# A second attention's threshold, search, product and loop order, rewritten

## The chip, the cores and the metric

The kernel runs on one core of one Trainium2 chip. The metric is device time in microseconds (us) of one execution, given as the median of several. All times, durations and waits below come from those runs or from one profiled execution of the kernel before.

The core has five engines that run beside each other, each through its own list of instructions in order: PE (TensorE, matrix products; its weight loads are listed apart as PEld), DVE (VectorE), ACT (ScalarE), POOL (GpSimd) and SP (SyncE, which here issues the transfers). [...] An instruction waits on semaphores for the results that it reads and for the space that it writes.

## What is computed

A graph of 1250 nodes with 512 features goes through a first graph layer, a first attention with experts, a second graph layer and a second attention. Only the second attention is changed. Its reference, cut to what matters:

```python
qkv = x @ qkv_w.T + qkv_b            # x: one sequence of 1250 rows, with positions added
q, k, v = jnp.split(qkv, [c, 2 * c], axis=-1)
q, k, v = (_split_heads(t, h) for t in (q, k, v))          # 8 heads of 64
logits = jnp.einsum('bmd,bpd->bmp', qd * scale, kd)
_, idx = lax.top_k(logits, TOPK)                           # TOPK = 16
k_sel, v_sel = gather(k, idx), gather(v, idx)
attn = jax.nn.softmax(jnp.einsum('bmd,bmkd->bmk', q * scale, k_sel), axis=-1)
out = jnp.einsum('bmk,bmkd->bmd', attn, v_sel)
...
return out @ wo_w.T + wo_b                                 # added to x
```

Each row of each head takes its sixteen largest of 1250 scores, and a softmax over those sixteen alone weighs the values.

## The kernel before

The first 1110 us of the execution hold the first three layers and the projections of the second attention. The change leaves them as they are. The second attention is a loop of 40 steps (`steps`): ten row tiles `i` of 125 rows, and for each four pairs `j` of heads. Within a step the two heads of the pair are a_ = 0 and a_ = 1. The order of the work is written out by hand, under `manual_schedule`: each engine runs its instructions in the order in which the loop's body calls the helpers. Three steps are in work at once: step n is scored and searched, step n-1 is weighted and transposed, step n-2 multiplies its values.

One head of one step goes this way:
- `scores1` (L1595): TensorE writes scores of 125 rows by 1250 columns into a PSUM tile S of three banks, in three pieces (512, 512 and 226 columns), two products each. There is one such tile for each a_, so the next step's scores can be written only when both readings by ScalarE (below) are through.
- `largest1` (L1602): VectorE searches S with fourteen MAX8 instructions, each over every fourteenth column (89 or 90), and keeps eight values of each: 112 candidates.
- `first1` (L1611, L1612): a MAX8 over the candidates gives the eight largest (`top[:, 0:8]`); `nm` is the negative of the largest.
- `weights1` (L1630): ScalarE writes e = exp(S - largest).
- `second1` (L1620 to L1624): the eight largest are replaced among the candidates, a second MAX8 gives ranks nine to sixteen, and `gap` and `below` make the threshold: the negative of the sixteenth score, raised by a margin of 2^-22 times the larger magnitude among ranks one and eight. `gap` and `below` each read two columns of SBUF.
- `select1` (L1637, L1640): ScalarE takes the sign of S + below (1 for the sixteen, -1 for the others; the sums of the signs are collected for a test at the end), and GpSimd multiplies e by it in place, all 1250 columns in one instruction.
- `turn1` and `keep1` (L1650, L1657): TensorE transposes the twenty 125x125 blocks of the two heads in five groups of four (group 2 holds two blocks of each head), and ScalarE copies each group out with a Relu, which sets the unwanted, now negative weights to zero.
- `values1`, `outputs1` (L1706, L1716): TensorE multiplies the transposed weights by the values, and ScalarE copies the result out.

Once in a row tile come other small works, spread over its four steps by c = n % 4: the sum of the sixteen exponentials and its inverse (`sums1` to `sums_keep1`, with `sums_over1` on VectorE, L1673 and L1674, and `sums_turn1` on TensorE, L1687), the scaling of the outputs (`scale1`, L1694, on GpSimd), the split of the next tile's queries into halves (`halves1`: ScalarE L1580, GpSimd L1581, two transfers on SP), and in each step a quarter of the output projection (`project1`, L1724, on TensorE), which `finish1` (L1732) adds to X on VectorE; a finished tile is sent out by a transfer on SP. Transposes, outputs, the projection and the sums' transposes share two PSUM banks (`ps_to1`), taken in turn.

In a step of before TensorE runs: value products of n-2 (first 0 to 8, in 32 recorded products), transposes 0 of n-1, the last value products, two score pieces of head 1, transposes 1, the last score piece of head 1, transposes 2, the projection, the first score piece of head 0 of n+1, transposes 3, its other two pieces, transposes 4. ScalarE runs: sign of head 1 (n-1), keep 0, outputs, exp of head 0, keep 1, sign of head 0, keep 2, halves or the sums' exp, keep 3, exp of head 1, keep 4. VectorE runs: search, `first1`, `second1` of head 0, then search, `finish1`, `first1`, `second1` of head 1. GpSimd runs the two products and the works named above.

Of the kernel before, what the change touches and what calls it, by code (L numbers as in the profile page):

```python
# [9 lines left out]
F32 = mybir.dt.float32  # L10
# [6 lines left out]
ALU = mybir.AluOpType  # L17
# [555 lines left out]
def tile_usual(ctx: ExitStack, tc: tile.TileContext, a: dict, out: bass.AP):  # L573
# [970 lines left out]


    TINY = 2.0 ** -22
    SEARCHED = 14
    wo_pool, wo_p = pool("wo", 1)
    w_o = wo_p.tile([128, K, D], F32, name="w_o1")
    nc.sync.dma_start(w_o, a["wo"].rearrange("(k p) f -> p k f", p=128))  # L1550
# [2 lines left out]
    with (  # L1553
# [42 lines left out]
                                     start=(x == 0), stop=(x == 1))  # L1596


        def largest1(n, a_):
            largest[n, a_] = at1.tile([P, SEARCHED, 8], F32, tag=f"largest{a_}", name="largest")  # L1600
            for k in range(SEARCHED):
                nc.vector.max(out=largest[n, a_][:, k, :], in_=score[n, a_][:, k:N:SEARCHED])  # L1602

        def first1(n, a_):
            i, j = steps[n]
            h = 2 * j + a_
            if h == 0:
                bests[i] = at1.tile([P, H, TOPK], F32, name="best")
            top = bests[i][:, h, :]
            nm = maxima[n, a_] = at1.tile([P, 1], F32, tag=f"nm{a_}", name="nm1")  # L1610
            nc.vector.max(out=top[:, 0:8], in_=largest[n, a_].rearrange("p g e -> p (g e)"))  # L1611
            nc.vector.tensor_scalar(nm, top[:, 0:1], -1.0, None, op0=ALU.mult)  # L1612

        def second1(n, a_):
            i, j = steps[n]
            top = bests[i][:, 2 * j + a_, :]
            gap = at1.tile([P, 1], F32, tag=f"gap{a_}", name="gap")
            below = belows[n, a_] = at1.tile([P, 1], F32, tag=f"below{a_}", name="below")
            rest = at1.tile([P, SEARCHED * 8], F32, name="rest")
            nc.vector.match_replace(out=rest, in_to_replace=top[:, 0:8],  # L1620
                                    in_values=largest.pop((n, a_)).rearrange("p g e -> p (g e)"), imm_value=LOWEST)
            nc.vector.scalar_tensor_tensor(gap, top[:, 7:8], -1.0, top[:, 0:1], op0=ALU.mult, op1=ALU.max)  # L1622
            nc.vector.max(out=top[:, 8:16], in_=rest)
            nc.vector.scalar_tensor_tensor(below, gap, TINY, top[:, 15:16], op0=ALU.mult, op1=ALU.subtract)  # L1624

        def weights1(n, a_):
            if n > last:
# [5 lines left out]
        def select1(n, a_):  # L1633
            if not 0 <= n <= last:
                return
            sg = at1.tile([P, N], F16, tag=f"sg{a_}", name="sg", bufs=1)
            nc.scalar.activation(sg, score.pop((n, a_))[:, :N], AF.Sign, bias=belows.pop((n, a_)),  # L1637
                                 accum_out=signs[:, 2 * n + a_ : 2 * n + a_ + 1])
            e = es[n, a_]
            (nc.vector if 2 * n + a_ == 2 * last + 1 else nc.gpsimd).tensor_mul(e, e, sg)  # L1640

        def turn1(n, g):
            if not 0 <= n <= last:
                return
            if g == 0:
                pTs[n] = at1.tile([P, 2 * T, P], F32, name="pT1")
            turned[n, g] = ps_to1.tile([128, 512], F32, tag="to", name="ps_t1")
            g0, g1 = GROUPS[g]
            for b in range(g0, g1):
                nc.tensor.transpose(turned[n, g][:P, span(b - g0, b - g0 + 1)],  # L1650
                                    es[n, b // T][:, span(b % T, b % T + 1)], ident[:P, :P])
# [41 lines left out]
        def scale1(i):  # L1693
            nc.gpsimd.tensor_mul(oTs[i], oTs[i], sums.pop(i))  # L1694

        def values1(n, t0, t1):
            if not 0 <= n <= last:
                return
            i, j = steps[n]
            if t0 == 0:  # L1700
                outs[n] = ps_to1.tile([128, 512], F32, tag="to", name="O")
            pT = pTs[n]
            for t in range(t0, t1):
                for a_ in range(2):
                    h = 2 * j + a_
                    nc.tensor.matmul(outs[n][a_ * DH : (a_ + 1) * DH, :P],  # L1706
                                     V[:, t, h * DH : (h + 1) * DH], pT[:, a_ * T + t, :],
                                     start=(t == 0), stop=(t == T - 1))
# [54 lines left out]
        with tc.manual_schedule():  # L1763
            nc.sync.dma_start(w_v, a["qkv"][:, 2 * D :].rearrange("(k p) f -> p k f", p=128))
            nc.sync.dma_start(v_b, bass.AP(tensor=a["v_b"].tensor, offset=a["v_b"].offset, ap=[[0, P], [1, D]]))
            for a_ in range(2):
                halves1(0, a_)
            scores1(0, 0, 0, 2, 1)
            for n in range(len(steps)):


                i, c = n // K - 1, n % K
                if i >= 0 and c == 3:
                    scale1(i)
                select1(n - 1, 1)
                largest1(n, 0)
                values1(n - 2, 0, 5)
                first1(n, 0)
                if n == 1:
                    keep_late1()  # L1780
                second1(n, 0)
                values1(n - 2, 5, 8)
                turn1(n - 1, 0)
                keep1(n - 1, 0)
                values1(n - 2, 8, T)
                scores1(n, 1, 1)
                scores1(n, 1, 0)
                outputs1(n - 2)
                if i >= 0 and c == 1:
                    sums_over1(i)  # L1790
                weights1(n, 0)
                if i >= 0 and c == 2:
                    sums_turn1(i)
                    sums_keep1(i)
                turn1(n - 1, 1)
                scores1(n, 1, 2)
                if n < 2:
                    values_late1(T - 3 + 2 * n)
                keep1(n - 1, 1)
                turn1(n - 1, 2)  # L1800
                if i >= 0 and c == 0:
                    sums1(i)
                if i >= 1:
                    project1(i - 1, c)
                select1(n, 0)
                largest1(n, 1)
                keep1(n - 1, 2)
                finish1()
                if c < 2:
                    halves1(steps[n][0] + 1, c)  # L1810
                if i >= 0 and c == 1:
                    sums_wide1(i)
                scores1(n + 1, 0, 0)
                if i >= 0 and c == 0:
                    sums_exp1(i)
                if n == 1:
                    keep_late1()
                turn1(n - 1, 3)
                keep1(n - 1, 3)
                first1(n, 1)  # L1820
                if n == 0:
                    keep_late1()
                scores1(n + 1, 0, 2)
                scores1(n + 1, 0, 1)
                if n == 0:
                    values_late1(T - 2)
                weights1(n, 1)
                turn1(n - 1, 4)
                keep1(n - 1, 4)
                second1(n, 1)  # L1830

            n, i = len(steps), T - 1
            sums1(i)
            values1(n - 2, 0, 5)
            select1(n - 1, 1)
            turn1(n - 1, 0)
            values1(n - 2, 5, T)
            keep1(n - 1, 0)  # L1840
            outputs1(n - 2)
            sums_exp1(i)
            turn1(n - 1, 1)
            keep1(n - 1, 1)
            sums_over1(i)
            sums_wide1(i)
            y0 = ps_s1a.tile([P, 3 * 512], F32, name="S")
            y1 = ps_s1b.tile([P, 3 * 512], F32, name="S")
            project1(i - 1, 0, D, y0[:, :D])
            turn1(n - 1, 2)  # L1850
            keep1(n - 1, 2)
            finish1()
            sums_turn1(i)
            sums_keep1(i)
            turn1(n - 1, 3)
            keep1(n - 1, 3)
            R = sums.pop(i)
            oT = oTs[i]
            nc.vector.tensor_mul(oT[:, : K - 1, :], oT[:, : K - 1, :], R[:, : K - 1, :])

            def terms(*ks):
                for k in ks:
                    nc.tensor.matmul(y1[:, :D], oT[:, k, :], w_o[:, k, :], start=(k == 0), stop=(k == K - 1))

            terms(0)
            turn1(n - 1, 4)
            signs_over1()
            terms(1)
            keep1(n - 1, 4)
            values1(n - 1, 0, T)  # L1870
            terms(2)
            nc.vector.tensor_mul(oT[:, K - 1, :], outs.pop(n - 1)[:, :P], R[:, K - 1, :])
            terms(K - 1)
            projected.append((i, slice(0, D), y1[:, :D]))
            finish1()
# [62 lines left out]
```

## Time and profile before

| | |
|---|---|
| median of 3 runs | 1533.59 us (1533.37 to 1535.1) |
| the profiled execution: its own time | 1535.23 us |
| its span | 1533.3 us |
| mean granted TensorE clock | 0.987 |
| from 1110 to 1512 us (402 us): PE, PEld busy | 367.5, 296.6 us |
| the same stretch: DVE, ACT, POOL busy | 380.6, 334.5, 243.9 us |

In a row of groups the profile gives line, engine, operation, what is written from what, shape and count; then the busy time of the group (overlaps counted once) and the mean duration of one; then the engine's idle time just before it and what ended it. In a timeline a row gives the start, the length and the count of merged instructions. Instructions of one engine overlap a little in it: the next one may start before the last one's end. A row of stretches gives busy time and count for each engine in turn. The busy share is an average over instructions that may stand still while they count as busy, and the ends of matrix products are modelled.

### The profile page before, as it was taken

How to read it: one execution, taken by the hardware profiler on the slowest of the kernel's cores; microseconds unless marked ns; L12 is line 12 of the kernel's file. 1: busy time of each engine (PE TensorE's matmuls, PEld its weight loads, DVE VectorE, ACT ScalarE, POOL GpSimd, SP SyncE). 2: the span in 40 equal slices, each digit the busy share in tenths (PEclk: the TensorE clock that was granted, in tenths of full speed). 3: DMA queues.
4: the chain of work that ended last, by engine and by line, in shares of the span. 5: the costliest groups of instructions: out<-in, count | busy, mean ns of one | idle time of the engine just before them, and what ended most of it. 6: DMA issues, size and time to landing. Idle time of an engine off the chain costs nothing.

```text
span 1533.3 us, 22442 instructions
## 1 busy us (share of the span) xinstructions
PE 1429.5 (93%) x8127; PEld 938.3 (61%) x8127; DVE 913.7 (60%) x2772; ACT 708.0 (46%) x1351; POOL 350.2 (23%) x301
## 2 busy tenths in 40 slices
PE   5999999979999998999999999989888999999997
PEld 3666744457777775444444446654467777777775
DVE  8895567544444332412222434654599999999995
ACT  2333434455455552211000123431178888888884
POOL 0110000001111120000000122210046666666652
PEclk9999999989999999999999999999999999999999
DMA  4001000010101000210000100000200000000000
GB/s 138 29 1 55 1 0 1 4 48 15 42 16 48 21 24 14 60 54 28 28 28 28 50 7 28 1 28 0 75 15 14 15 22 22 22 22 22 22 8 23
DMA packets 42331, 41.19 MB, mean 27 GB/s; under 512 B 25738, under 2 KB 30084, under 8 KB 42211
## 3 DMA queue, kind: packets, MB, share of 16 engines
q1 hardware_dynamic: 42211, 39.66, 9.0%
q8 instruction: 66, 1.08, 0.3%
q14 instruction: 54, 0.44, 0.1%
HBM read 26.81 MB, written 2.56 MB: 19 GB/s over the span
## 4 chain that ended last, share of the span: by engine, by line
PE 59%; DVE 30%; ACT 8%; issue 2%; DMA 0%; POOL 0%; DVEq 0%; ACTq 0%; SPq 0%
PE ps_o L1334 9%; DVE largest L1602 9%; PE ps_mm L1326 7%; DVE gap L1622 5%; PE ps_mm L865 5%; PE ps_mm L800 5%; PE S L1034 4%; PE ps_mm L1462 4%; PE ps_o L870 4%; PE ps_t L1122 4%; PE O L1143 3%; PE bank L768 2%; PE O L1187 2%; DVE below L1624 2%; PE S L1157 1%
## 5 line engine op out<-in xcount | busy, mean ns | idle before, releaser
L1640 POOL TENSOR_TENSOR e<-e,sg 125x1250 f32<-125x1250 f32 x79 | 203.3, 2573 | 157.2 <-ACT sg L1637 105.6
L1602 DVE MAX8 largest<-S 125x8 f32<-125x89 f32 (+1 forms) x1120 | 183.3, 239 | 3.8 <-PE S L1595 3.8
L1336 DVE SCALAR_TENSOR_TENSOR X<-ps_o,gate,X 125x512 f32<-125x512 f32 x80 | 60.0, 750 | 177.0 <-PE ps_o L1334 177.0
L1595 PE MATMUL S<-K,stacks 128*125 128x512 f32 x480 | 135.7, 394 | 24.5 <-ACT sg L1637 19.0
L1650 PE MATMUL ps_t<-ident,e 125*125 125x125 f32 x800 | 136.3, 288 | 14.1 <-POOL e L1640 6.8
L1650 PEld LDWEIGHTS ps_t<-ident,e 125*125 125x125 f32 x800 | 111.9, 191 | 48.5 <-ACT pT L1657 14.5
L1334 PE MATMUL ps_o<-we,hid 128*125 128x512 f32 x320 | 141.2, 595 | 0.0
L1657 ACT ACTIVATE pT<-ps_t 125x500 f32<-125x500 f32 x200 | 117.0, 585 | 33.6 <-PE ps_t L1650 31.7
L1329 ACT ACTIVATE hid<-ps_mm,b 128x500 f32<-128x500 f32 (+1 forms) x40 | 24.6, 614 | 209.0 <-PE ps_mm L1326 209.0
L1326 PE MATMUL ps_mm<-yT,we 128*128 128x500 f32 (+1 forms) x320 | 115.8, 520 | 0.0
L1630 ACT ACTIVATE e<-S,nm 125x1250 f32<-125x1250 f32 x80 | 104.1, 1302 | 18.1 <-DVE nm L1612 17.9
L1637 ACT ACTIVATE sg<-S,below 125x1250 f16<-125x1250 f32 x80 | 104.4, 1305 | 16.4 <-DVE below L1624 12.9
L1706 PE MATMUL O<-pT,yT 125*64 125x125 f32 x1600 | 105.0, 276 | 0.2 <-ACT pT L1657 0.2
L1334 PEld LDWEIGHTS ps_o<-we,hid 128*125 128x125 f32 x320 | 59.0, 187 | 72.4 <-issue 69.6
L1595 PEld LDWEIGHTS S<-K,stacks 128*125 128x125 f32 x480 | 73.9, 194 | 44.3 <-ACT sg L1637 30.2
L1127 ACT COPY pT<-ps_t 125x500 f32<-125x500 f32 (+3 forms) x112 | 54.7, 489 | 93.2 <-PE ps_t L1122 92.2
L1622 DVE SCALAR_TENSOR_TENSOR gap<-best 125x1 f32<-125x1 f32 x80 | 95.8, 1197 | 0.0
L1326 PEld LDWEIGHTS ps_mm<-yT,we 128*128 128x128 f32 x320 | 60.2, 189 | 55.2 <-issue 53.3
L1706 PEld LDWEIGHTS O<-pT,yT 125*64 125x64 f32 x1600 | 86.1, 137 | 10.7 <-DVE bad L1760 0.8
L1034 PE MATMUL S<-K,stacks 128*125 128x512 f32 (+10 forms) x288 | 84.1, 400 | 7.0 <-ACT e L1101 6.5
L1122 PE MATMUL ps_t<-ident,e 125*125 125x125 f32 x440 | 81.5, 296 | 9.5 <-ACT pT L1127 6.0
L640 ACT ACTIVATE rs<-rs 125x1 f32<-125x1 f32 x60 | 12.1, 203 | 164.0 <-DVE rs L639 160.7
(240 smaller groups left out, 2559.7 us busy)
## 6 DMA issues: line engine op xcount, KB each, us to landing
we<-in_W SPq DMA_DIRECT2D x16, 512.0 KB
stacks<-stacks SPq DMA_DIRECT2D x160, 31.2 KB
stacks<-stacks SPq DMA_DIRECT2D x40, 125.0 KB
X<-in_x SPq DMA_DIRECT2D x5, 500.0 KB
out<-y SPq DMA_DIRECT2D x10, 250.0 KB
w_n<-in_wn SPq DMA_DIRECT2D x1, 1024.0 KB
w_c<-in_wc SPq DMA_DIRECT2D x1, 1024.0 KB
w_q<-in_Wq SPq DMA_DIRECT2D x1, 1024.0 KB
```

Source lines behind the costliest of these rows:

```text
L1034: nc.tensor.matmul(ps[:, n0:w], stacks[n][:, x, a_, :], K2[:, 2 * j + a_, n0:w], start=(x == 0), stop=(x == 1))
L1122: nc.tensor.transpose(ps[:P, span(t - t0, t - t0 + 1)], es[n, a_][:, span(t, t + 1)], ident[:P, :P])
L1326: nc.tensor.matmul(ps[:, :n], w1[:, k, f * 128 : (f + 1) * 128], yT[:, k, span(t0, t1)], start=(k == 0), stop=(k == K - 1))
L1334: nc.tensor.matmul(ps[:P], hid[:, f, span(t, t + 1)], w2[:, f, :], start=(f == 0), stop=(f == FF // 128 - 1))
L1595: nc.tensor.matmul(score[n, a_][:, n0:n1], stacks[i][:, x, h, :], K2[:, h, n0:n1], start=(x == 0), stop=(x == 1))
L1602: nc.vector.max(out=largest[n, a_][:, k, :], in_=score[n, a_][:, k:N:SEARCHED])
L1622: nc.vector.scalar_tensor_tensor(gap, top[:, 7:8], -1.0, top[:, 0:1], op0=ALU.mult, op1=ALU.max)
L1637: nc.scalar.activation(sg, score.pop((n, a_))[:, :N], AF.Sign, bias=belows.pop((n, a_)), accum_out=signs[:, 2 * n + a_ : 2 * n + a_ + 1])
L1640: (nc.vector if 2 * n + a_ == 2 * last + 1 else nc.gpsimd).tensor_mul(e, e, sg)
L1650: nc.tensor.transpose(turned[n, g][:P, span(b - g0, b - g0 + 1)], es[n, b // T][:, span(b % T, b % T + 1)], ident[:P, :P])
L1657: nc.scalar.activation(pTs[n][:, g0:g1, :], turned.pop((n, g))[:P, : (g1 - g0) * P].rearrange("p (t n) -> p t n", n=P), AF.Relu)
L1706: nc.tensor.matmul(outs[n][a_ * DH : (a_ + 1) * DH, :P], V[:, t, h * DH : (h + 1) * DH], pT[:, a_ * T + t, :], start=(t == 0), stop=(t == ...
```

## The change

The margin of the threshold is now 2^-22 of the sixteenth score's own magnitude: `gap` and `below` give way to two `tensor_scalar` operations on that score, into the two columns of a small tile, and a `tensor_reduce` that takes the larger. The search is made in two parts: the first 1024 columns in twelve MAX8, the last 226 in three, so 120 candidates in place of 112. GpSimd's product (VectorE's, for the very last head) is issued in two pieces: 500 and 750 columns for head 0, 250 and 1000 for head 1, cut where a group of transposes ends. And the loop's body calls the helpers in another order: on TensorE the projection comes ahead of transposes 2; on VectorE the search's second part comes first for head 0 and last for head 1, and `sums_over1` comes ahead of `first1`; on GpSimd `scale1` comes behind the product of head 1; on ScalarE the sums' exp comes ahead of the halves. The remaining lines move in the text but keep their place on their engine.

```diff
--- before.py
+++ after.py
@@ -1544,7 +1544,8 @@
     TINY = 2.0 ** -22
-    SEARCHED = 14
+    SEARCHED = ((0, 1024, 12), (1024, N, 3))
+    FOUND = sum(x[2] for x in SEARCHED) * 8
     wo_pool, wo_p = pool("wo", 1)
     w_o = wo_p.tile([128, K, D], F32, name="w_o1")
     nc.sync.dma_start(w_o, a["wo"].rearrange("(k p) f -> p k f", p=128))
@@ -1596,10 +1597,13 @@
                                      start=(x == 0), stop=(x == 1))
-        def largest1(n, a_):
-            largest[n, a_] = at1.tile([P, SEARCHED, 8], F32, tag=f"largest{a_}", name="largest")
-            for k in range(SEARCHED):
-                nc.vector.max(out=largest[n, a_][:, k, :], in_=score[n, a_][:, k:N:SEARCHED])
+        def largest1(n, a_, part):
+            if (n, a_) not in largest:
+                largest[n, a_] = at1.tile([P, FOUND], F32, tag=f"largest{a_}", name="largest")
+            n0, n1, step = SEARCHED[part]
+            for k in range(step):
+                c = part * SEARCHED[0][2] + k
+                nc.vector.max(out=largest[n, a_][:, 8 * c : 8 * c + 8], in_=score[n, a_][:, n0 + k : n1 : step])
         def first1(n, a_):
             i, j = steps[n]
@@ -1608,20 +1612,22 @@
                 bests[i] = at1.tile([P, H, TOPK], F32, name="best")
             top = bests[i][:, h, :]
             nm = maxima[n, a_] = at1.tile([P, 1], F32, tag=f"nm{a_}", name="nm1")
-            nc.vector.max(out=top[:, 0:8], in_=largest[n, a_].rearrange("p g e -> p (g e)"))
+            nc.vector.max(out=top[:, 0:8], in_=largest[n, a_])
             nc.vector.tensor_scalar(nm, top[:, 0:1], -1.0, None, op0=ALU.mult)
         def second1(n, a_):
             i, j = steps[n]
             top = bests[i][:, 2 * j + a_, :]
-            gap = at1.tile([P, 1], F32, tag=f"gap{a_}", name="gap")
             below = belows[n, a_] = at1.tile([P, 1], F32, tag=f"below{a_}", name="below")
-            rest = at1.tile([P, SEARCHED * 8], F32, name="rest")
+            rest = at1.tile([P, FOUND], F32, name="rest")
             nc.vector.match_replace(out=rest, in_to_replace=top[:, 0:8],
-                                    in_values=largest.pop((n, a_)).rearrange("p g e -> p (g e)"), imm_value=LOWEST)
-            nc.vector.scalar_tensor_tensor(gap, top[:, 7:8], -1.0, top[:, 0:1], op0=ALU.mult, op1=ALU.max)
+                                    in_values=largest.pop((n, a_)), imm_value=LOWEST)
             nc.vector.max(out=top[:, 8:16], in_=rest)
-            nc.vector.scalar_tensor_tensor(below, gap, TINY, top[:, 15:16], op0=ALU.mult, op1=ALU.subtract)
+
+            sides = at1.tile([P, 2], F32, tag=f"sides{a_}", name="sides")
+            nc.vector.tensor_scalar(sides[:, 0:1], top[:, 15:16], -1.0 + TINY, None, op0=ALU.mult)
+            nc.vector.tensor_scalar(sides[:, 1:2], top[:, 15:16], -1.0 - TINY, None, op0=ALU.mult)
+            nc.vector.tensor_reduce(below, sides, AX.X, ALU.max)
         def weights1(n, a_):
             if n > last:
@@ -1637,7 +1643,10 @@
             nc.scalar.activation(sg, score.pop((n, a_))[:, :N], AF.Sign, bias=belows.pop((n, a_)),
                                  accum_out=signs[:, 2 * n + a_ : 2 * n + a_ + 1])
             e = es[n, a_]
-            (nc.vector if 2 * n + a_ == 2 * last + 1 else nc.gpsimd).tensor_mul(e, e, sg)
+
+            engine = nc.vector if 2 * n + a_ == 2 * last + 1 else nc.gpsimd
+            for c in (slice(0, (4, 2)[a_] * P), slice((4, 2)[a_] * P, N)):
+                engine.tensor_mul(e[:, c], e[:, c], sg[:, c])
         def turn1(n, g):
             if not 0 <= n <= last:
@@ -1770,64 +1779,66 @@
                 i, c = n // K - 1, n % K
-                if i >= 0 and c == 3:
-                    scale1(i)
+                values1(n - 2, 0, 5)
+                values1(n - 2, 5, 8)
+                turn1(n - 1, 0)
+                largest1(n, 0, 1)
                 select1(n - 1, 1)
-                largest1(n, 0)
-                values1(n - 2, 0, 5)
+                largest1(n, 0, 0)
+                if i >= 0 and c == 1:
+                    sums_over1(i)
+                values1(n - 2, 8, T)
                 first1(n, 0)
                 if n == 1:
                     keep_late1()
-                second1(n, 0)
-                values1(n - 2, 5, 8)
-                turn1(n - 1, 0)
                 keep1(n - 1, 0)
-                values1(n - 2, 8, T)
+                if i >= 0 and c == 3:
+                    scale1(i)
                 scores1(n, 1, 1)
                 scores1(n, 1, 0)
                 outputs1(n - 2)
-                if i >= 0 and c == 1:
-                    sums_over1(i)
                 weights1(n, 0)
                 if i >= 0 and c == 2:
                     sums_turn1(i)
                     sums_keep1(i)
                 turn1(n - 1, 1)
+                second1(n, 0)
+                if i >= 0 and c == 0:
+                    sums1(i)
+                largest1(n, 1, 0)
                 scores1(n, 1, 2)
                 if n < 2:
                     values_late1(T - 3 + 2 * n)
+                if i >= 1:
+                    project1(i - 1, c)
                 keep1(n - 1, 1)
                 turn1(n - 1, 2)
-                if i >= 0 and c == 0:
-                    sums1(i)
-                if i >= 1:
-                    project1(i - 1, c)
                 select1(n, 0)
-                largest1(n, 1)
-                keep1(n - 1, 2)
+                scores1(n + 1, 0, 0)
+                largest1(n, 1, 1)
                 finish1()
-                if c < 2:
-                    halves1(steps[n][0] + 1, c)
-                if i >= 0 and c == 1:
-                    sums_wide1(i)
-                scores1(n + 1, 0, 0)
-                if i >= 0 and c == 0:
-                    sums_exp1(i)
                 if n == 1:
                     keep_late1()
                 turn1(n - 1, 3)
-                keep1(n - 1, 3)
+                scores1(n + 1, 0, 2)
                 first1(n, 1)
                 if n == 0:
                     keep_late1()
-                scores1(n + 1, 0, 2)
+                second1(n, 1)
+                keep1(n - 1, 2)
                 scores1(n + 1, 0, 1)
                 if n == 0:
                     values_late1(T - 2)
+                turn1(n - 1, 4)
+                if i >= 0 and c == 0:
+                    sums_exp1(i)
+                if c < 2:
+                    halves1(steps[n][0] + 1, c)
+                keep1(n - 1, 3)
+                if i >= 0 and c == 1:
+                    sums_wide1(i)
                 weights1(n, 1)
-                turn1(n - 1, 4)
                 keep1(n - 1, 4)
-                second1(n, 1)
```

## The prediction

> **What bounds the kernel now.** I read the busy shares first, then the second attention alone by stretches, its groups, its chain of waits, and last the order of instructions on VectorE and GpSimd. The page gives whole-kernel shares, and they mislead: TensorE leads.
>
> ```profile
> PE 1429.5 (93%) x8127; PEld 938.3 (61%) x8127; DVE 913.7 (60%) x2772; ACT 708.0 (46%) x1351; POOL 350.2 (23%) x301
> ```
>
> The changed stage is the loop of 40 steps (two heads each), from the first search at 1110.96 to the tail at 1511. There the busy times per stretch of 40 us read
>
> ```profile
> 1280.00:1320.00 40.00, 36.54 (x326) 29.85 (x326) 38.36 (x176) 33.63 (x53) 25.23 (x14) 1.00 0.09 21
> 1320.00:1360.00 40.00, 37.12 (x331) 30.37 (x331) 38.28 (x177) 34.26 (x54) 25.54 (x14) 1.00 0.09 21
> ```
>
> (columns: stretch, PE, PEld, DVE, ACT, POOL, granted clock, DMA share, GB/s). DVE has 38.3 of 40, and its 1120 searches waited 3.8 us in all, so DVE sets the pace; but PE (37.1) and ACT (34) stand close behind. The groups of the stage say what DVE does:
>
> ```profile
> L1602 DVE MAX8 largest<-S 125x8 f32<-125x89 f32 (+1 forms) x1120 | 183.3, 239 | 3.8 <-PE S L1595 3.8
> L1622 DVE SCALAR_TENSOR_TENSOR gap<-best 125x1 f32<-125x1 f32 x80 | 95.8, 1197 | 0.0
> L1624 DVE SCALAR_TENSOR_TENSOR below<-gap,best 125x1 f32<-125x1 f32 x80 | 35.3, 441 | 6.8
> L1640 POOL TENSOR_TENSOR e<-e,sg 125x1250 f32<-125x1250 f32 x79 | 203.3, 2573 | 157.2 <-ACT sg L1637 105.6
> ```
>
> An operation on one element per partition takes 1197 ns. By its own line it ranges 150/1204/2457 ns (least, median, most), so it stands still for something. VectorE and GpSimd side by side in time (start, duration):
>
> ```profile
> 1300.85 0.15 DVE L1612 TENSOR_SCALAR nm<-best 125x1 f32<-125x1 f32 x1
> 1300.92 0.08 DVE L1620 MATCH_VALUE_LOAD rest<-best,largest 125x8 f32 x1
> 1300.99 0.26 DVE L1620 MATCH_REPLACE8 rest<-best,largest 125x112 f32<-125x112 f32 x1
> 1301.17 1.41 DVE L1622 SCALAR_TENSOR_TENSOR gap<-best 125x1 f32<-125x1 f32 x1
> 1302.50 0.27 DVE L1623 MAX8 best<-rest 125x8 f32<-125x112 f32 x1
> 1302.87 0.92 DVE L1624 SCALAR_TENSOR_TENSOR below<-gap,best 125x1 f32<-125x1 f32 x1
> 1303.71 0.41 DVE L1602 MAX8 largest<-S 125x8 f32<-125x90 f32 x2
> ```
>
> ```profile
> 1299.99 2.57 POOL L1640 TENSOR_TENSOR e<-e,sg 125x1250 f32<-125x1250 f32 x1 [2.23 <-ACT sg L1637]
> 1302.51 1.25 POOL L1694 TENSOR_TENSOR oT<-oT,R 128x500 f32<-128x500 f32 x1
> ```
>
> `gap` ends at 1302.58, as the GpSimd product ends (1302.56); `below` ends at 1303.79, as the next GpSimd operation does (1303.76). Both read two SBUF operands and stand until GpSimd is through. `nm`, with one operand, takes 0.15 in the middle of the same product. That is the cost the change aims at.
>
> **VectorE's step now and after.** From the search of head 0 in step 9 (1204.05) to that in step 39 (1500.13) are 30 steps, 9.87 us each. From the start of the replace to the next search, one half step now takes 0.17 + 1.12 (`gap`, less its overlap of 0.08) + 0.34 (second MAX8 and hand-off) + 0.36 (mean `below` 0.441, less 0.08) = 1.99. (Twice 2.32 of search, 0.49 of `first1` and 1.99, with 0.19 for the add of `finish1` and 0.11 for the sums, is 9.9: no slack.) Afterwards: the MAX8 must wait for the replace alone, 0.26 + 0.10 hand-off = 0.36; then 0.34; two `tensor_scalar` and a `tensor_reduce` in place of `below`. The nearest row for the first two is `nm`, 154 ns, whose independent follower starts 0.07 later; for the reduce, L1673 (125x128, 280 ns) above and the free `gap` (150 ns) below; I take 0.18. So 0.07 + 0.22 (154 ns and a hand-off) + 0.10 (0.18 less the overlap) = 0.39, and 1.09 in all: 0.90 less. The search scans the same 1250 columns in 15 instead of 14 instructions: between nothing and one more spacing (2.29/14 = 0.16); MAX8 takes 276 ns over 112 columns and 239 over 90, 1.7 a column, so most of a spacing is scan; I take 0.07. Three reads of 120 instead of 112 columns: about 0.01. **Net 0.82 per half step, 1.64 per step, VectorE's step 8.23 us.**
>
> The two-sided bound: if no new operation ever stands, 0.82; if the first `tensor_scalar` stands as `gap` did, it costs 1.05 more and 0.82 becomes a loss of 0.23. [...]
>
> ```profile
> L1612 DVE TENSOR_SCALAR nm<-best x80: 153/154/156, 1113.6 to 1507.5; 125x1 f32<-125x1 f32 x80
> ```
>
> 80 of 80 at 153 to 156 ns, inside GpSimd products too. [...]
>
> **What is late next: TensorE and ScalarE.** TensorE's step, packed, by starts of weight loads (a step around 1390.26 to 1400 us): fifth transposes 0.69, 32 value products 1.87, first transposes 0.63, 8 value products 0.58, scores 0.80, second transposes 0.56, scores 0.21, third transposes 0.63, projection 1.12, scores 0.48, fourth transposes 0.43, scores 0.57: 8.57, plus 0.56 once in four steps for the sums' transposes: **8.7**. A check by waits, from 1180 to 1500 (32.4 steps): weight loads waited 21.3 us for the sign, 10.7 for GpSimd, 6.3 for R; 38.3/32.4 = 1.18, and 9.87 - 1.18 = 8.7. The granted clock is 1.00 at 37 busy of 40, so I put nothing for it.
> ScalarE: two signs at 1.29 (with the accumulator's read), two exps at 1.20, five keeps at 0.49, a copy 0.20: 7.63, plus 0.25 (halves, in half of the steps), 0.08 (sums' exp) and 0.11 (R): 8.1. GpSimd: 25.4/40 of 9.87 = 6.3.
> A ring joins them: first transposes, keep (0.55), copy (0.30), exp (1.20), keep (0.49), sign (1.30), hand-off (0.1): 3.95; then on TensorE scores 0.48, fourth transposes 0.43, scores 0.57, fifth transposes 0.6, value products 1.87, first transposes 0.63: 4.6. Sum 8.55, about 8.7 with R's copy once in four. Three lanes at 8.2 to 8.7, tied together, do not run at the largest of them: I add 0.2 for hand-offs. **Step 8.9, saving 0.97.**
>
> **The other edits.** The product in two pieces: GpSimd's rows of 128 columns (400 ns) and 1250 (2573) give 1.94 ns a column and 0.15 fixed, so 0.15 more per head, 0.3 a step: GpSimd at 6.6 of 8.9, hidden; if its cover went, 12 us in all. In return the first transposes may start after 500 (or 250) columns, 1.5 us sooner: that takes the 10.7 us of waits for GpSimd, counted above. The search in two parts lets VectorE start before the last score piece: worth nothing while it is late, up to 0.3 when it waits, counted in the 8.9. Moved: `scale1` on GpSimd behind the product of head 1 (1.25 us in one step of four, its reader a row later): 0. `halves1` behind the sums' exp on ScalarE (0.3 once in four; its subtraction and two transfers on SP follow, needed steps later): 0. `sums_over1` ahead of `first1` on VectorE: 0.41 on one exp in four, which in the ring waits for the copy until later anyway: 0. The projection ahead of the third transposes: 1.1 us more for GpSimd's product, but the fourth transposes then need the bank that `finish1` frees, and that add is queued on VectorE behind both searches of head 1. With VectorE's search at 0, the add ends at about 6.5; TensorE comes to the fourth transposes at about 6.8: slack 0.3, cost 0, at most 0.5 if it turns.
>
> **The sum.** Steps 0 and 1 are filled by late value products on TensorE and give 0.3 each; 37 steps × 0.97 = 35.9; the tail loses one `gap` wait but ends on other chains, 0: 36.5. The profiled execution took 1535.23 (span 1533.3, 1.9 around it), so 1498.7; it lay 1.64 above the median of 1533.59, so **1497**.
>
> **Rivals.**
> A, a wait takes its place: the bank behind `finish1`, or a hand-off in the ring, costs about 0.5 a step: 9.4, 37 × 0.47 = 17, 1516. For it: the slack of 0.3; against: VectorE is now early. Chance 0.21.
> B, TensorE packs to its sum: 8.55, 37 × 1.32 = 49, 1484 or a little less. For it: the transposes' earlier start; against: three lanes within 0.5. 0.10.
> C, no change: the ring itself takes 9.8 already. Against: PE waits 1.2 us per step for results that VectorE's stalls make late. 0.04.
> D, slower: the first `tensor_scalar` stands behind GpSimd's product as `gap` does. Loss 0.23 × 80 = 18 us: 1552. It decides from a mean of about 0.97 us (0.15 + 0.82) of that instruction; against it stands L1612. 0.05.
>
> **How the numbers follow.** The forecast (1486 to 1507) has 0.60. Faster 0.91, within 0.2% (what a measurement of this kernel can tell from no change) 0.04, slower 0.05. The range takes in most of A and B: 1480 to 1520.
>
> **What would show it.** Both new `tensor_scalar` at about 0.15 and the reduce at 0.15 to 0.2, with no long ones; VectorE's busy share in the loop down from 0.96 to about 0.83, with waits for the scores; PE near 0.97 or above; searches of head 0 every 8.9 us; few waits of transposes for GpSimd. Wrong: long `tensor_scalar`; fourth transposes waiting for the add of `finish1`; a lower granted clock as TensorE fills.

## The result, and the profile after

The changed kernel takes 1548.93 us (median of 4 runs, 1547.97 to 1550.54) against 1534.34 for the kernel before on the same chip: ratio 1.0096, 95% interval 1.0078 to 1.0113. It is slower by 1%, where 2.4% faster was forecast, and outside the range. The profiled execution took 1550.54 us (span 1548.7). Line numbers below are those of the kernel a row comes from; the searches are L1602 before and L1606 after, the scores L1595 and L1596.

First the busy shares of the whole span, then two of the stretches of 40 us in the loop (columns as before):

```profile
PE 1417.9 (92%) x8127; PEld 938.9 (61%) x8127; DVE 845.2 (55%) x2933; ACT 711.2 (46%) x1351; POOL 362.8 (23%) x380
```

```profile
1280.00:1320.00 40.00, 33.99 (x313) 29.20 (x308) 30.21 (x185) 33.04 (x52) 26.40 (x21) 1.00 0.08 19
1320.00:1360.00 40.00, 33.98 (x320) 29.16 (x319) 30.21 (x186) 33.13 (x51) 25.77 (x21) 1.00 0.08 18
```

VectorE fell from 38.3 to 30.2 of 40 us, as meant. But no engine took its place: TensorE fell too, from 37 to 34, ScalarE from 34 to 33, and GpSimd, at 26, is far from full. Every engine has room here and the loop is slower, so I looked for engines that wait for each other in turn. The groups of the loop:

```profile
L1606 DVE MAX8 largest<-S 125x8 f32<-125x85 f32 (+3 forms) x1200 | 193.4, 235 | 61.7 <-PE S L1596 61.5
L1596 PE MATMUL S<-K,stacks 128*125 128x512 f32 x480 | 134.3, 390 | 66.9 <-DVE largest L1606 62.8 <-DVE yT L1483 4.2
L1630 DVE TENSOR_REDUCE below<-sides 125x1 f32<-125x2 f32 x80 | 12.4, 155 | 6.1
L1628 DVE TENSOR_SCALAR sides<-best 125x1 f32<-125x1 f32 x80 | 12.3, 154 | 2.8
L1629 DVE TENSOR_SCALAR sides<-best 125x1 f32<-125x1 f32 x80 | 11.5, 144 | 0.0
```

The stall is gone: the three new operations take 154, 144 and 155 ns in place of 1197 and 441. In the first two rows stands the news: the scores wait 62.8 us for the search, and the search 61.5 us for the scores. In the kernel before, the scores waited for the sign and at the loop's start for the values (`yT`), not for the search:

```profile
L1595 PE MATMUL S<-K,stacks 128*125 128x512 f32 x480 | 135.7, 394 | 24.5 <-ACT sg L1637 19.0 <-DVE yT L1483 4.2
```

By time the changed loop looks like this, on TensorE and on VectorE:

```profile
1364.17 1.19 PE L1596 MATMUL S<-K,stacks 128*125 128x512 f32 x4
1365.20 0.60 PE L1659 MATMUL ps_t<-ident,e 125*125 125x125 f32 x4
1367.40 0.48 PE L1596 MATMUL S<-K,stacks 128*125 128x226 f32 x2 [1.60 <-DVE largest L1606]
1367.71 1.04 PE L1733 MATMUL O<-w_o,oT 128*125 128x128 f32 x8
```

```profile
1365.40 1.94 DVE L1606 MAX8 largest<-S 125x8 f32<-125x86 f32 x12 [0.48 <-PE S L1596]
1367.92 0.53 DVE L1606 MAX8 largest<-S 125x8 f32<-125x76 f32 x3 [0.57 <-PE S L1596]
```

The last score piece of head 1 (226 columns) starts at 1367.40, just after the twelve MAX8 over the first 1024 columns end (1367.34). It writes none of the columns that they read. TensorE stands 1.60 us for it (1.17 in one step of four), and everything behind it in TensorE's list stands too: projection, transposes, the next step's scores. A step, by the starts of `nm` from step 9 to step 39, is 10.22 us (before: 9.87).

### The profile page after: what moved, and what is told of

Its sections match the earlier page's. It is cut to its first block, busy times and chain, and to the rows that moved or that the text cites. A ratio compares the mean times of both kernels' runs of the same rounds, so it can differ in the third digit from the quotient of the medians.

```text
span 1548.7 us, 22735 instructions
## 1 busy us (share of the span) xinstructions
PE 1417.9 (92%) x8127; PEld 938.9 (61%) x8127; DVE 845.2 (55%) x2933; ACT 711.2 (46%) x1351; POOL 362.8 (23%) x380
## 4 chain that ended last, share of the span: by engine, by line
PE 74%; DVE 15%; ACT 8%; issue 2%; DMA 0%; POOL 0%; ACTq 0%; SPq 0%; DVEq 0%
PE ps_o L1334 9%; PE ps_mm L1326 7%; PE S L1596 7%; PE O L1715 6%; DVE largest L1606 5%; PE ps_mm L865 5%; PE ps_t L1659 5%; PE ps_mm L800 4%; PE S L1034 4%; PE ps_mm L1462 4%; PE ps_o L870 4%; PE ps_t L1122 4%; PE O L1143 3%; PE bank L768 2%; PE O L1187 2%
## 5 line engine op out<-in xcount | busy, mean ns | idle before, releaser
L1649 POOL TENSOR_TENSOR e<-e,sg 125x500 f32<-125x500 f32 (+3 forms) x158 | 214.6, 1380 | 154.6 <-PE ps_t L1659 65.9
L1606 DVE MAX8 largest<-S 125x8 f32<-125x85 f32 (+3 forms) x1200 | 193.4, 235 | 61.7 <-PE S L1596 61.5
L1596 PE MATMUL S<-K,stacks 128*125 128x512 f32 x480 | 134.3, 390 | 66.9 <-DVE largest L1606 62.8
L1596 PEld LDWEIGHTS S<-K,stacks 128*125 128x125 f32 x480 | 72.7, 190 | 87.1 <-DVE largest L1606 70.8
L1659 PE MATMUL ps_t<-ident,e 125*125 125x125 f32 x800 | 124.1, 277 | 0.8 <-ACT pT L1666 0.7
L1715 PE MATMUL O<-pT,yT 125*64 125x125 f32 x1600 | 109.0, 276 | 0.5
L1122 PE MATMUL ps_t<-ident,e 125*125 125x125 f32 x440 | 81.7, 296 | 9.5 <-ACT pT L1127 6.0
L1005 POOL TENSOR_TENSOR stacks<-yT,stacks 64x125 fp32r<-64x125 f32 x80 | 34.2, 428 | 232.1 <-ACT stacks L1004 228.7
```

The source lines that it names most:

```text
L1122: nc.tensor.transpose(ps[:P, span(t - t0, t - t0 + 1)], es[n, a_][:, span(t, t + 1)], ident[:P, :P])
L1596: nc.tensor.matmul(score[n, a_][:, n0:n1], stacks[i][:, x, h, :], K2[:, h, n0:n1], start=(x == 0), stop=(x == 1))
L1606: nc.vector.max(out=largest[n, a_][:, 8 * c : 8 * c + 8], in_=score[n, a_][:, n0 + k : n1 : step])
L1649: engine.tensor_mul(e[:, c], e[:, c], sg[:, c])
L1715: nc.tensor.matmul(outs[n][a_ * DH : (a_ + 1) * DH, :P], V[:, t, h * DH : (h + 1) * DH], pT[:, a_ * T + t, :], start=(t == 0), stop=(t == ...
```

## Experiments

Ratios are to the kernel before on the same chip, with 95% intervals. **Theory W**: in the text of the changed loop the search of head 1's first part is called ahead of the head's last score piece, and that alone makes the score piece wait for the search. **Theory R**: TensorE, ScalarE and their hand-offs are the limit, the wait shows only where the slack lies.

**One line moved in the text.**

```diff
-                largest1(n, 1, 0)
                 scores1(n, 1, 2)
+                largest1(n, 1, 0)
```

> The kernel after with one line moved in the text: the last score piece of head 1 is called ahead of the search of head 1's first part. Every engine's list of instructions stays the same; only the waits can differ. Theory W (the search called first makes the last score piece wait for the end of the twelve MAX8, a write after a read of the same PSUM tile, 1.6 us a step): the wait goes, a step falls from 10.25 to 8.7 to 9.0 us, and the time to about 1490 to 1503. Theory R (TensorE, ScalarE and the hand-offs are the limit, the wait for the search only where the slack shows): no change beyond 5 us of 1549.

1508.22 us, ratio 0.983 (0.9815 to 0.9845): 41 us less than the changed kernel, with every engine's list the same, instruction for instruction. The same place on TensorE:

```profile
1364.25 1.20 PE L1596 MATMUL S<-K,stacks 128*125 128x512 f32 x4
1365.30 0.60 PE L1659 MATMUL ps_t<-ident,e 125*125 125x125 f32 x4
1365.65 0.46 PE L1596 MATMUL S<-K,stacks 128*125 128x226 f32 x2
1365.95 1.04 PE L1733 MATMUL O<-w_o,oT 128*125 128x128 f32 x8
```

No wait for the search is left. W holds; R falls. The time came 5 us above W's span: the step is 9.24, not 8.7 to 9.0. Of the wait, 1.49 us a step on average (40.1 us in 27 steps), 0.98 came back as time; 0.37 a step (11.0 us in 30) is now a wait for the sign of head 0, a little later in TensorE's list.

**The new threshold alone, on the kernel before** (`second1` as in the change, all else as before).

> The kernel before with the new threshold alone (two one-operand operations and a reduce in place of gap and below). Theory W: VectorE's step falls from 9.87 by about 1.7 us and no new wait comes, so TensorE and ScalarE bound the step at about 9 us: 1495 to 1507. Theory R: the freed time is lost in hand-offs, 1525 or more. If the new operations stood behind GpSimd: above 1534.

1506.09 us, 0.9815 (0.98 to 0.9829), the lowest median of all. The step is 9.18 us. One of its stretches and two of its waits (who waited for whom: us in total, times, longest; 1200 to 1480 us):

```profile
1280.00:1320.00 40.00, 39.38 (x350) 32.52 (x351) 30.74 (x190) 36.90 (x58) 27.64 (x14) 1.00 0.10 24
```

```profile
DVE largest L1602 <- PE S L1595: 39.6, 31, 1.9
PEld S L1595 <- ACT sg L1638: 9.6, 30, 0.3
```

This is the picture that was forecast for the change: TensorE busy 39.4 of 40, VectorE with slack and waiting for scores. But the second wait recurs in every step: TensorE's weight loads stand for the sign, so TensorE is not quite full (more on it below).

**The search in two parts alone, on the kernel before.** `largest1` as in the change, and

```diff
                 turn1(n - 1, 1)
+                largest1(n, 1, 0)
                 scores1(n, 1, 2)
...
-                largest1(n, 1)
+                largest1(n, 1, 1)
```

> The kernel before with the search in two parts alone, head 1's first part called ahead of its last score piece, as in the kernel after; the stalling threshold stays. Theory W: the same wait appears; VectorE, still the bound, now idles about 0.6 us a step between its two parts, and has one more MAX8 per head: slower by 20 to 30 us, 1555 to 1565. Theory R: slower by the additional MAX8 alone, 5 us, 1540.

1622.34 us, 1.057 (1.0552 to 1.0588): the wait is there, and the kernel loses 87 us, three to four times what W said. I had counted VectorE's short idle between its parts. But the score piece's wait ends on VectorE behind the stalling threshold of head 0, so the stalls are in TensorE's list as well, and the wait is longer (62.5 us in 23 steps, 2.72 each). Up to about 37 of the 87 us may be a lower TensorE clock, 0.965 on average against 0.987 before (an estimate, last section). One such wait:

```profile
1373.70 0.48 PE L1596 MATMUL S<-K,stacks 128*125 128x226 f32 x2 [2.73 <-DVE largest L1606]
```

**Contiguous runs in the changed kernel**: each MAX8 takes a run of about 85 columns, not every twelfth; the calls stay.

```diff
-in_=score[n, a_][:, n0 + k : n1 : step]
+in_=score[n, a_][:, n0 + k * (n1 - n0) // step : n0 + (k + 1) * (n1 - n0) // step]
```

> The kernel after with each MAX8 over a contiguous run of about 85 columns in place of every twelfth one, same calls in the same order. If the wait comes from the strided reads reaching, by count times step, past column 1024: it goes, and the time falls to about 1497. If it is kept for the whole PSUM tile, or for whatever was called first: the wait stays at 1.6 us a step and the time at 1549.

The kernel went on to its general program behind the loop (it does when the sums of the signs at the end do not come out), so its whole time, 4116.94 us, tells nothing here; the loop's rows do. From 1200 to 1480 us the scores wait 40.1 us in 27 steps for the search, as in the changed kernel, and a single wait is the same to 0.01 us:

```profile
1367.91 0.48 PE L1596 MATMUL S<-K,stacks 128*125 128x226 f32 x2 [1.59 <-DVE largest L1606]
```

So the strides, which might seem to reach past column 1024, are not the cause.

**A PSUM tile of its own for the last piece of head 1**, in the changed kernel, with the calls in its order; ScalarE needs two exps and two signs for that head.

```diff
-                score[n, a_] = ps_s1[a_].tile([P, 3 * 512], F32, name="S")
+                score[n, a_] = ps_s1[a_].tile([P, (3, 2)[a_] * 512], F32, name="S")
+                ends[n, a_] = ps_s1c.tile([P, 512], F32, name="S2") if a_ else score[n, a_][:, 1024:]
```

> The kernel after, its calls in the same order, with the last 226 score columns of head 1 in a PSUM tile of their own (ScalarE then needs two exps and two signs for head 1, about 0.5 us more a step). If the wait belongs to the tile as a whole, whatever its columns: TensorE no longer waits for the search, and the step is bound by ScalarE and TensorE at 9.2 to 9.6 us: 1515 to 1532. If the wait has another cause (the order of the calls alone, the bank, the engine): it stays, 1549 or more.

1510.82 us, 0.9842 (0.9828 to 0.9855); no wait of the scores for the search, though the search is still called first:

```profile
1368.11 0.60 PE L1673 MATMUL ps_t<-ident,e 125*125 125x125 f32 x4
1368.46 0.46 PE L1601 MATMUL S<-K,stacks 128*125 128x226 f32 x2
```

The wait belongs to the tile: in this program the write into S that was called behind the twelve reads of S waited for them (1.60 us, 1.17 in one step of four), though they read other columns, and the same write into a tile of its own did not (other tiles were not tried). A place apart inside S is not enough, for the last piece had columns 1024 to 1249 to itself before as well. The time was better than expected, since the extra exps and signs cost ScalarE only 7 us of the 280 from 1200 to 1480 (260 busy, 253 with the one line moved).

**The old threshold in the changed kernel** (`gap` and `below` back, the rest as changed).

> The kernel after with gap and below back in place of the new threshold. If the wait for the search hides VectorE's stalls (the step is TensorE's list plus 1.6 us, VectorE has slack): 1549 to 1560. If VectorE's chain is in the same ring, the stalls come on top of it: 1600 to 1630, near the kernel before with the parts alone (1622).

1609.12 us, 1.0483 (1.0468 to 1.0497). With the wait in place the stalls cost 60 us (1609 to 1549), without it 29 (1535 to 1506). TensorE's wait for the search grew from 1.49 to 2.37 us a step (56.9 us in 24 steps), so VectorE's delays do reach TensorE's list through it. But the granted clock fell too (0.93 from 1200 to 1480 us, 1.00 in the changed kernel), and up to about 28 of the 60 us may be that (an estimate, last section): how much dearer the wait itself makes the stalls is not shown.

**The other edits.** The product in two pieces, on the kernel before with the new threshold:

> The kernel before with the new threshold and the product in two pieces, old loop and search in one part. With the new threshold alone the transposes waited 2.0 us for GpSimd in 280 us, so the pieces have nothing left to win and their 0.3 us a step lies beside TensorE: 1504 to 1508, as with the threshold alone (1506). If the product was still a bound: 1500 or less.

1507.44 us, 0.9818 (0.9805 to 0.9832): nothing, as said. The order of the loop alone, on the kernel before (search in one part, called behind its scores):

> The kernel before with the new order of the loop alone (search in one part, called behind the head's last score piece; stalling threshold, product in one piece). Theory W: VectorE is the bound as before and the order has no wait of its own: 1528 to 1540. If the order itself carries the loss: 1545 or more.

1537.12 us, 1.0014 (1.0007 to 1.002): 2 us slower; the order itself carries nothing of the gain and little of the loss. The search in two parts, called behind its scores, with the new threshold on the kernel before:

> The kernel before with the new threshold and the search in two parts, head 1's first part called behind its last score piece. Theory W: no wait for the search; the fifteenth MAX8 lies on a VectorE with slack: 1505 to 1509, as with the threshold alone (1506). If splitting the search costs by itself: 1512 or more.

1510.41 us, 0.9837 (0.9823 to 0.985). It is 4 us above the threshold alone, but the intervals overlap, so a small price of splitting is possible and not shown. The projection moved back behind the third transposes, in the run with the one line moved:

> The run that called the last score piece first (1508) with the projection moved back behind the third transposes. There TensorE waited 0.43 us a step for the sign of head 0 and was busy 38.5 of 40 us, against 39.4 with the threshold alone. If the place of the projection makes that wait (the keep of the second transposes and with it the sign come later on ScalarE): 1503 to 1506. If it lies in the other edits (two pieces, two parts): 1508.

1509.2 us, 0.9827 (0.9813 to 0.984). TensorE's idle time before the scores that waited for the sign (11.0 us of 280) went, and its busy time rose from 267.9 to 275.1 us. The time did not move. The weight loads of these scores still wait for the sign in every step (10.0 us in 30 steps; 16.7 with the projection in front): the sign comes no sooner, and the projection only fills the time before it. So my reading of that wait as the projection's cost was wrong, and TensorE's busy share, whose ends are modelled, was no measure of it.

## Why the prediction was wrong

- **The stall.** Right. Of the 80 `gap` in the kernel before 77 took over 200 ns, and each of these ended 13 to 22 ns after a GpSimd operation did. The new forms do not stand: the first `sides` shows 153/154/157 ns (least, median, most), and of the 160 `tensor_scalar` of both kinds more than 130 lie wholly inside a GpSimd product, none over 157 ns. The reduce, of which no row stood in the profile before, shows 154/155/158. As the row of `nm` had said (76 of its 80 lie wholly inside a GpSimd operation, none over 156 ns), a `tensor_scalar` on one column did not stand here, and rival D fell with it. From the start of the replace to the next search 1.09 us were forecast; the run with the threshold alone has 1.00 where that search need not wait (1368.34 to 1369.34).
- **The step that failed** is the sentence on the search in two parts: "worth nothing while it is late, up to 0.3 when it waits". I looked at each engine's list and asked what each waits for in the data. The lists do keep their order; the waits follow the order of the calls and the tile (1549 us; 1508 with one call moved and every list the same, 1511 with a tile of its own). The part called ahead of a score piece turns that piece into a write behind a read: 1.60 us on TensorE in three steps of four and 1.17 in the fourth, a term that the sum had at nothing. Moving the call takes 41 us off: without the wait the change gains 27 us (1535 to 1508), with it it loses about 14.
- The other half of that idea, that VectorE starts head 0 on its small part before the last piece is written, brings nothing either: in the changed kernel that search starts at 1370.82, when all three pieces are there (the four products from 1369.86 end at 1370.79).
- **The size of the new step.** Forecast 8.9; with the wait gone 9.24, with the threshold alone 9.18. The prediction had TensorE packed (8.7) and the ring through ScalarE (8.55) side by side and added 0.2. The trace speaks for the ring. One turn of it in the run with the threshold alone, on TensorE, ScalarE (first transposes' keep, then the sign) and TensorE again:

```profile
1360.46 1.94 PE L1707 MATMUL O<-pT,yT 125*64 125x125 f32 x32
1362.32 0.70 PE L1651 MATMUL ps_t<-ident,e 125*125 125x125 f32 x4
```

```profile
1363.06 0.59 ACT L1658 ACTIVATE pT<-ps_t 125x500 f32<-125x500 f32 x1 [0.33 <-PE ps_t L1651]
1365.68 1.30 ACT L1638 ACTIVATE sg<-S,below 125x1250 f16<-125x1250 f32 x1
1366.87 0.20 ACT L1638 ACTIVATION_READ_ACCUMULATOR sg<-S,below 125x1 f32 x1
```

```profile
1367.12 0.29 PEld L1595 LDWEIGHTS S<-K,stacks 128*125 128x125 f32 x2 [0.34 <-ACT sg L1638]
1369.35 1.94 PE L1707 MATMUL O<-pT,yT 125*64 125x125 f32 x32
```

  From that keep to the end of the sign ScalarE does not wait again, and the weight load at 1367.12 has waited for the sign. The parts were forecast at 2.50 (products and first transposes), 3.95 (ScalarE and hand-off) and 2.08 (scores and transposes); they measure 2.60, 4.06 and 2.23, so 8.89 in all against 8.55. The products of four steps in a row start 8.89, 9.16, 8.90 and 9.77 us apart; the last step holds the transposes of the sums and the copy of their inverses (the tile R), 0.8 more than the others. This also fits the run with the projection moved back, where TensorE's busy time grew and the step stayed at 9.24. No run shortens the ring alone, so that it is the bound is read from the trace and not tested. The saving is 0.69 a step, not 0.97, and 29 us, not 36.5.
- **Rival A** named a wait in TensorE's list, but at the bank behind `finish1`. No fourth transposes waited for it. **B** and **C** fell with the step of the threshold alone: 9.18 is neither 8.55 nor 9.8. The loss has the sign of D and nothing of its cause; that D's 1552 lies near the 1549 measured is chance.
- **Moved works** at 0: held (2 us in all for the order). **Two pieces** at 0 with GpSimd hidden: held.

## What to carry to other kernels

Before costing a reordering, list for each moved call not only its place on its engine, but which tile it reads or writes and which calls on the same tile it now stands ahead of or behind: a read called ahead of a write to the same tile was a wait of 1.17 to 1.60 us here, though the columns differed and the lists of the engines stayed. When the leading engines all lose busy time and the kernel slows, look for two groups that wait for each other (62.8 and 61.5 us here). To overlap parts of one buffer, try tiles of their own for the parts (1511 us here, against 1549), or call the writes first (1508). And a busy share near 1 (39.4 of 40 us with the threshold alone) did not name the bound: look which waits recur in every step.

## What the runs showed of the hardware

The granted TensorE clock fell in the loops where TensorE stood longest, though it then had less to do. In the changed kernel (27 waits of 1.49 us on average, the longest 1.6) it is 1.00 from 1200 to 1480 us; with the parts alone (23 waits of 2.72 us on average, the longest 3.3) a stretch reads

```profile
1240.00:1280.00 40.00, 31.80 (x279) 27.79 (x280) 31.18 (x151) 27.99 (x42) 20.42 (x12) 0.92 0.07 18
```

and from 1200 to 1480 us it is 0.93 with the old threshold in the changed kernel (24 waits of 2.37 us on average, the longest 3.7). The length of a wait does not decide: with the parts alone waits of 2.85 and 2.36 us were followed by a fall to 0.50, of 2.88 and 2.48 not. In the traces of the kernel before and of the changed kernel the granted clock changes only at times a whole number of 3.41 us apart, and the falls in the loops go with how busy TensorE was in the last such interval (its ends are modelled). Two pairs of neighbours at that spacing, with the parts alone:

```profile
1358.97:1362.38 3.41, 1.47 (x13) 1.47 (x14) 2.41 (x16) 1.91 (x4) 1.81 (x1) 1.00 0.00 0
1362.38:1365.80 3.42, 3.42 (x14) 3.03 (x14) 1.50 (x8) 1.97 (x5) 1.77 (x2) 0.50 0.25 56
...
1369.21:1372.62 3.41, 1.76 (x12) 1.26 (x8) 3.27 (x11) 3.32 (x5) 1.72 (x1) 1.00 0.00 0
1372.62:1376.04 3.42, 2.34 (x19) 2.25 (x20) 2.04 (x12) 1.47 (x4) 2.58 (x2) 1.00 0.01 2
```

The wait of 2.83 us that ends at 1360.91 lies mostly in one interval; the wait of 2.73 us that ends at 1373.70 is divided at 1372.62. In that run's intervals from 1243 to 1291 us and from 1359 to 1383 us the three falls follow 1.05, 1.24 and 1.47 us of TensorE busy, and none follows 1.76 or more. In the loop of the kernel before the four falls follow 1.36, 1.41, 1.58 and 1.83 us, while in the changed kernel intervals with 1.81 us are followed by none: no one busy time divides the two. At 0.50 two score products of 512 columns take 1.20 in place of 0.71 us:

```profile
1362.53 1.20 PE L1596 MATMUL S<-K,stacks 128*125 128x512 f32 x2
...
1375.25 0.71 PE L1596 MATMUL S<-K,stacks 128*125 128x512 f32 x2
```

What this costs can only be estimated, from the mean granted clock and the span of the profiled executions. What the clock lacks of 1.00, times the span, is 56.7 us with the parts alone (0.965, 1620.3 us) and 19.9 before (0.987, 1533.3 us): at most about 37 of the 87 us. It is 49.8 us with the old threshold in the changed kernel (0.969, 1607.8 us) and 21.7 in the changed kernel (0.986, 1548.7 us): at most about 28 of the 60 us. No run has these waits without the falls.
